# Narrower TensorE tiles, two running totals and split transfers in a kernel of attention, windowed attention and two convolutions

## The chip, the cores and the metric

The kernel runs on one core of a Trainium2 chip. The metric is the device time of one execution in microseconds (us). Before the change the median of three runs is 2969.88 us (2968.04 to 2971.42).

## The reference

Two layers work on `x` of shape (2, 256, 64, 64), in float32. The first is full attention over the 4096 positions of an image, with 8 heads of 32 channels, and a fusion that a mask blends with the input:

```python
attn = softmax(einsum('bnd,bmd->bnm', q / sqrt(32), k))
fuse = einsum('bnm,bmd->bnd', attn, v)
hybrid = conv1x1(concat([x, fuse]), Wf, bf)
x = hybrid * m + x * (1 - m)
```

The second layer has a channel gate, attention inside windows of 8x8 positions (4 heads of 64 channels) with an output projection and a residual, a shuffle of the channels, two grouped 7x7 convolutions (four channels into one, one into four) with normalisation, and a gate:

```python
x = x * sigmoid(relu(x @ ca_w1 + ca_b1) @ ca_w2 + ca_b2)
x = x + (softmax(qw @ kw.T / 8) @ vw) @ out_w + out_b     # per window
y = relu(bn1(conv7x7(shuffle(x), sa_w1)))                 # 64 groups
x = shuffle(x) * sigmoid(bn2(conv7x7(y, sa_w2)))          # 64 groups
```

## The kernel before, in words

**First part (lines 366 to 507).** It projects q, k and v for 16 chunks of 512 positions (8 a image) and keeps them in DRAM, and prepares the banded weights of the two convolutions, the mask and the constants. This part isn't changed.

**Attention (the loop at 1163).** It has 1024 slots: image b, chunk c, half g of the heads (4 heads each), block m of 128 keys (32 blocks). In a slot TensorE makes the scores of the slot two ahead (`scores`, 626: eight matmuls in tiles of 32 rows by 64 columns, written 32*64), ScalarE takes their exponentials in three instructions (639) into a buffer `e` (8 of them), TensorE multiplies the slot's exponentials by the values (`products`, 658: four matmuls in tiles of 128*32 side by side, summed in PSUM over the 32 blocks), and VectorE adds the exponentials to a running total (660). An fp32 matmul stands in the trace as two records, one for each pass. `products` ends a half with a copy of its sum (668). The list `later` holds what is due some slots after: DN = 8 slots after a chunk's end the `denominators` (681: totals times ones, in 128*32), then the reciprocal (706), four transfers of the inverse to DRAM (693) and eight that spread it back over partitions (699), all on GpSimd's queue, and the product with the sum (710).

**The stage of a chunk (`stage`, 714)** is a generator of some dozen pieces. The loop runs one piece every fourth slot, right after a slot's products: fusion with the input (725, first half from `x`, second half from the attention's `f`), `ca1` and `ca2` of the channel gate (754, 768), two q/k projections (796), window scores (830), the v projection (882), transposes (905), outputs (924), the output projection (946), and the sum that goes to DRAM as rows of `x_s` (972) for the convolutions. Fusion, q/k, v and output projection use tiles of 128*128, ca1 128*64. The stages of chunks 0 to 14 run within attention, that of chunk 15 after it.

**Convolutions (`convolve`, 985)**, also a generator. `items` lists 24 pieces of work: 8 groups of channels of image 0 (items 0 to 7, the early ones, whose rows are in DRAM before the end of attention), 6 of image 1 (8 to 13), 8 of both images at once, "pairs" (14 to 21), and two more of image 1. An item loads weights (1010) and rows (1017) on SyncE's queue, makes the first convolution (1038, 56 matmul records, 128*32) and its relu (1046), the second one (1062, 56 records, 32*128, reading weights with a stride of seven elements), tanh and scaling on ScalarE (1072, 1078) into a buffer `z` (two of them), the gate (1084, VectorE), and 12 stores an image (1097). The stores go to GpSimd and SyncE in turn; those of items 4 to 7, once the last stage is through (`staged`), go to GpSimd alone, and those of the last item to ScalarE and SyncE. One step of the generator is a second convolution, or a gate with the first convolution two items on. The order at the end of attention: first convolutions of items 0 and 1, denominators, second convolution of item 0, then the stage of chunk 15 with one convolution step after each piece that says so (`yield True`), then the rest of the items (1193 to 1204).

[...] A second branch of the program, for large scores, isn't taken with these inputs.

Of the kernel before, what the change touches and what calls it, by code (L numbers as in the profile page):

```python
# [10 lines left out]
F32 = mybir.dt.float32  # L11
# [37 lines left out]
UW = UG * KS  # L49
EPS = 1e-5  # L50
SCALE0 = 1.0 / math.sqrt(HD0)

# [4 lines left out]
def conv_seq_kernel(ctx: ExitStack, tc: tile.TileContext, a, out):  # L57
# [37 lines left out]
    for h in range(HEADS0):  # L95
# [12 lines left out]
    inv_s = {  # L108
        (b, c): dram.tile([HEADS0, CH], F32, name=f"invs_{b}_{c}")
        for b in range(B)  # L110
# [403 lines left out]


    def pipeline(arm, shifted, pools):
        fp, xpool, gp, wp, avp, ctx_conv = pools
# [129 lines left out]
        def products(i):  # L647
            b, c, g, m = slots[i]
            if m == 0:
                acc[0] = avp.tile([P, CH], F32, tag="av", name=f"av{arm}_{i}")  # L650
                acc[1] = ep.tile([P, HG, CH], F32, tag="sum", name=f"sum{arm}_{i}", bufs=3)
                totals[b, c, g] = acc[1]
            av, total = acc[0], acc[1]
            e, v = es[i], vts[b, c, g, m // PB]
            start, stop = m == 0, m == NMB - 1
            for j in range(HG):
                r = slice(32 * j, 32 * j + 32)
                nc.tensor.matmul(av[r, :], v[:, m % PB, r], e[:, j, :], start=start, stop=stop)  # L658
            if m > 0:
                nc.vector.tensor_add(total, first[0] if m == 1 else total, e)  # L660
            e = es.pop(i)
            if start:
                first[0] = e
            if stop:
# [25 lines left out]

                def store_inv():
                    for q in range(4):
                        nc.gpsimd.dma_start(  # L693
                            inv_s[b, c][:, q * P : (q + 1) * P], inv[32 * q : 32 * q + HEADS0]
                        )

                def spread(gg):
                    for h in range(HG):
                        nc.gpsimd.dma_start(  # L699
                            rd[32 * h : 32 * h + 32, gg].rearrange("p q n -> p (q n)"),  # L700
                            inv_s[b, c][HG * gg + h].partition_broadcast(32),
                        )
# [3 lines left out]
                at(DN + 1, lambda: nc.vector.reciprocal(inv, inv))  # L706
                at(DN + 1, store_inv)
                for gg in range(KC):
                    at(DN + 1, lambda gg=gg: spread(gg))
                at(DN + 7 + late, lambda: nc.vector.tensor_mul(f, f, rd.rearrange("p g q n -> p g (q n)")))  # L710
# [3 lines left out]
        def stage(b, c):  # L714
# [7 lines left out]
            for half in range(2):  # L722
                for oc in range(KC):
                    for kc in range(KC * half, KC * half + KC):
                        nc.tensor.matmul(  # L725
                            s[:, oc, :],
                            wf[:, kc, oc * P : (oc + 1) * P],
                            f[:, kc - KC, :] if half else xw[kc],
                            start=(kc == 0),
                            stop=(kc == 2 * KC - 1),  # L730
                        )
# [20 lines left out]
            for kc in range(KC):  # L752
                for h in range(2):
                    nc.tensor.matmul(
                        s[64 * h : 64 * h + 64, 0, 0:half],
                        cw1[:, kc, :],
                        x1[:, kc, toks[h]],
                        start=(kc == 0),
                        stop=(kc == KC - 1),
                    )  # L760
# [30 lines left out]
            def project(hc):  # L791
                s = psum2(f"qk{tag}_{hc}")
                for j in range(2):
                    o = (KC * j + hc) * P
                    for kc in range(KC):
                        nc.tensor.matmul(  # L796
                            s[:, j, :],
                            wqkv[:, kc, o : o + P],
                            u[:, kc, :],
                            start=(kc == 0),  # L800
                            stop=(kc == KC - 1),
                        )
# [77 lines left out]
            for t in range(4):  # L880
                for kc in range(KC):
                    nc.tensor.matmul(  # L882
                        sv[:, t, :],
# [60 lines left out]
            for oc in range(KC):  # L944
                for kc in range(KC):
                    nc.tensor.matmul(  # L946
                        s[:, oc, :],
# [34 lines left out]
        items += [(u, (0, 1)) for u in range(EARLY, NU)] + [(1, (1,)), (0, (1,))]  # L982
        staged = []

        def convolve():
            nb = len(BLOCKS)


            early, xcs, ycs = [], [], []
            for k in range(4):  # L990
                early.append(cpool.tile([P, nb, UG, WP], F32, name=f"xe{arm}{k}"))
            for k in range(2):
# [60 lines left out]
            def conv2(k):  # L1053
# [5 lines left out]
                for d in range(KS):  # L1059
                    for j in range(4):  # L1060
                        r = slice(32 * j, 32 * j + 32)
                        nc.tensor.matmul(  # L1062
                            tiles[j // 2][:, j % 2, 0 : n * W],
                            w[r, d],
                            y[r, 0:n, d : d + W],
                            start=(d == 0),
                            stop=(d == KS - 1),
                        )
                z = pool.tile([P, 4, B * nb * W], F32, tag="z", name=f"z{arm}{k}", bufs=2)
                z = z[:, :, 0 : n * W]  # L1070
                for hh in range(2):
                    nc.scalar.activation(  # L1072
                        z[:, 2 * hh : 2 * hh + 2, :],
                        tiles[hh][:, :, 0 : n * W],
                        AF.Tanh,
                        scale=0.5,
                    )
                nc.scalar.activation(z, z, AF.Copy, bias=0.25, scale=0.25)  # L1078
                return z.rearrange("p j (n x) -> p j n x", x=W)

            def gate(k, z):
                u, images = items[k]
                x = xs[k][:, 0 : nb * len(images), :, PAD : PAD + W]
                nc.vector.tensor_mul(z, z, x.rearrange("p n g x -> p g n x"))  # L1084

                engines = (nc.gpsimd, nc.sync)
                if k == len(items) - 1:
                    engines = (nc.scalar, nc.sync)
                elif staged and k < EARLY:
                    engines = (nc.gpsimd,)  # L1090
                stores = 0
                for m, b in enumerate(images):
                    for n, (x0, r0, r1) in enumerate(BLOCKS):
                        for i in range(4):
                            p = 32 * i + 1 - x0
                            stores += 1
                            engines[stores % len(engines)].dma_start(  # L1097
                                dst[b, i, r0:r1, UG * u : UG * u + UG, :],
                                z[p + r0 : p + r1, :, nb * m + n, :],
                            )  # L1100


# [60 lines left out]
        for i, (b, c, g, m) in enumerate(slots):  # L1163
            now[0] = i
            if (b, c, g, m) == (B - 1, NCHUNK - 1, 0, 0):
                for _ in banded:
# [27 lines left out]
        while later:  # L1194
            now[0] += 1
            run_later()
            if now[0] == len(slots) + DN:
                next(conv)
# [91 lines left out]
```

## Time and profile before

| | |
|---|---|
| median of three runs | 2969.88 us |
| the profiled execution | 2969.57 us |
| its span (first to last instruction) | 2967.5 us |
| granted TensorE clock, mean | 0.995 |
| last records of attention's products | 2729.4 us after the start |
| end of the output projection of chunk 15 | 2797.3 us |
| end of the last second convolution | 2954.6 us |

The page of a profile gives, for each engine, its busy time, the chain of work that ended last, and groups of equal instructions: line, engine, operation, written and read tiles, shape, count, then busy time in us and the mean of one in ns, and the idle time of the engine just before them with what ended it. PE is TensorE's matmuls, PEld its weight loads, DVE VectorE, ACT ScalarE, POOL GpSimd, SP SyncE, and SPq its queue. The timeline merges neighbours: start and length in us, and how many records; in brackets the idle time before. Ends of matmuls are modelled, so the starts are read: the distance from one group's start to the next one's is what a group takes. The tail's order on the page:

```profile
PE   9999999999999999999999999999999999999997
...
PEclk9999999999999999999999999999999999999998
DMA  8545421322242324242322223232323232422564
GB/s 248 199 165 172 128 70 53 85 68 78 56 89 63 89 60 89 63 79 70 75 71 68 77 64 75 60 85 62 88 63 74 73 83 66 109 69 78 152 197 103
```

Each of the 40 slices is 74 us: TensorE is busy throughout, and transfers matter at both ends only.

### The profile page before, as it was taken

What the parts mean: (1) busy time and instruction counts of PE and PEld (TensorE: products, weight loads), DVE (VectorE), ACT (ScalarE), POOL (GpSimd) and SP (SyncE); (2) the same over time, 40 slices, a digit from 0 to 9 for tenths busy, and PEclk for the clock granted to TensorE, in tenths of its full rate; (3) what the DMA queues carried; (4) which work ended last, traced back from release to release, by engine and by line L of the source; (5) the groups of instructions that cost most, each with busy time, mean ns of one, the idle gap of its engine ahead of it and who ended that gap; (6) DMA issues with size and microseconds to landing.
All of it is one profiled execution on the core that took longest, in us unless ns stands there. A gap on an engine that the chain in (4) does not pass through costs nothing.

```text
span 2967.5 us, 77160 instructions
## 1 busy us (share of the span) xinstructions
PE 2927.6 (99%) x33162; PEld 915.5 (31%) x33162; DVE 2502.4 (84%) x1348; ACT 2459.3 (83%) x4119; POOL 361.9 (12%) x658
## 2 busy tenths in 40 slices
PE   9999999999999999999999999999999999999997
PEld 3551222222222222222222222222222222223775
DVE  3349999999999999999999999999999999998211
ACT  5569889898989898989989898989898998987333
POOL 8010000000010101010100000010101010000456
PEclk9999999999999999999999999999999999999998
DMA  8545421322242324242322223232323232422564
GB/s 248 199 165 172 128 70 53 85 68 78 56 89 63 89 60 89 63 79 70 75 71 68 77 64 75 60 85 62 88 63 74 73 83 66 109 69 78 152 197 103
DMA packets 230160, 275.74 MB, mean 93 GB/s; under 512 B 116968, under 2 KB 134204, under 8 KB 229552
## 3 DMA queue, kind: packets, MB, share of 16 engines
q1 hardware_dynamic: 200880, 231.47, 27.2%
q0 software_dynamic: 24560, 36.53, 6.0%
q8 instruction: 263, 4.31, 0.6%
q10 hardware_dynamic: 4368, 2.70, 0.3%
q14 instruction: 89, 0.73, 0.1%
HBM read 221.88 MB, written 66.39 MB: 97 GB/s over the span
## 4 chain that ended last, share of the span: by engine, by line
PE 92%; DVE 3%; POOL 2%; DMA 1%; ACT 1%; issue 1%; SPq 0%; DVEq 0%; ACTq 0%; POOLq 0%
PE sa L626 35%; PE ava L658 33%; PE qka L796 4%; PE hya L725 4%; PE q L427 2%; PE vwa L882 2%; DVE suma L660 2%; PE k L427 2%; PE opa L946 2%; PE v L464 2%; POOL out_dram L1097 2%; PE c2a L1062 1%; PE dna L681 1%; DMA out_dram<-za 1%; PE c1a L1038 1%
## 5 line engine op out<-in xcount | busy, mean ns | idle before, releaser
L660 DVE TENSOR_TENSOR suma<-suma,ea 128x2048 f32<-128x2048 f32 x960 | 2198.8, 2290 | 89.9 <-ACT ea L639 3.7
L639 ACT ACTIVATE ea<-sa 128x512 f32<-128x512 f32 (+1 forms) x3072 | 2038.0, 745 | 66.2 <-PE sa L626 25.6
L626 PE MATMUL sa<-qa,ka 32*64 32x512 f32 x16384 | 1157.2, 613 | 1.5 <-ACT vst L472 1.2
L658 PE MATMUL ava<-ea,va 128*32 128x512 f32 x8192 | 1091.2, 605 | 1.3 <-ACT fa L668 0.3
L626 PEld LDWEIGHTS sa<-qa,ka 32*64 32x64 f32 x16384 | 247.5, 129 | 784.5 <-ACT ea L639 718.2
L658 PEld LDWEIGHTS ava<-ea,va 128*32 128x32 f32 x8192 | 161.5, 108 | 834.4 <-issue 805.4
L972 POOL DMA_DIRECT2D xs<-xo x94 | 66.3, 712 | 1718.2 <-DVE xo L957 1713.7
L1097 POOL DMA_DIRECT2D out_dram<-za x210 | 117.8, 569 | 82.4 <-DVE za L1084 56.7
L1084 DVE TENSOR_TENSOR za<-za,xla 128x768 f32<-128x768 f32 (+1 forms) x16 | 21.7, 1359 | 115.6 <-ACT za L1078 75.8
L796 PE MATMUL qka<-ua,qkv_w 128*128 128x512 f32 x256 | 118.4, 605 | 0.0
L660 DVE TENSOR_TENSOR suma<-ea,ea 128x2048 f32<-128x2048 f32 x32 | 73.0, 2283 | 51.3 <-ACT ea L639 51.3
L693 POOL DMA_DIRECT2D invs<-inva x64 | 32.7, 518 | 659.2 <-DVE inva L706 486.3
L1062 PE MATMUL c2a<-yca,wa 32*128 32x192 f32 (+1 forms) x1344 | 101.0, 443 | 8.8 <-ACT za L1072 8.8
L1072 ACT ACTIVATE za<-c2a 128x384 f32<-128x384 f32 (+1 forms) x48 | 26.2, 595 | 97.0 <-DMA out_dram<-za 71.9
L733 ACT ACTIVATE ta<-hya,bf 128x512 f32<-128x512 f32 x32 | 20.2, 683 | 103.7 <-PE hya L725 97.5
L446 DVE TENSOR_REDUCE top<-sq 128x512 f32<-128x2048 f32 x16 | 36.6, 2285 | 79.0 <-ACT sq L440 79.0
L1062 PEld LDWEIGHTS c2a<-yca,wa 32*128 32x128 f32 x1344 | 92.0, 315 | 19.4 <-issue 9.6
L851 ACT ACTIVATE ewa<-ewa,mxwa 128x64 f32<-128x64 f32 x256 | 85.2, 347 | 1.5 <-DVE mxwa L842 1.5
L809 ACT ACTIVATE qka<-qka,qkv_b 128x512 f32<-128x512 f32 x64 | 40.4, 683 | 42.1 <-PE qka L796 41.7
L796 PEld LDWEIGHTS qka<-ua,qkv_w 128*128 128x128 f32 x256 | 46.0, 189 | 71.3 <-issue 46.1
L699 POOL DMA_DIRECT2D rda<-invs x128 | 63.3, 502 | 30.5 <-DMA invs<-inva 30.5
L427 PE MATMUL q<-x,WqT 128*128 128x512 f32 x128 | 61.0, 620 | 5.4 <-DMA WqT<-in_WqT_dram 5.4
(135 smaller groups left out, 1540.5 us busy)
## 6 DMA issues: line engine op xcount, KB each, us to landing
ka<-ks SPq DMA_DIRECT2D x256, 256.0 KB
va<-vs SPq DMA_DIRECT2D x256, 256.0 KB
wa<-ws SPq DMA_DIRECT2D x17, 896.0 KB
ws<-zeros SPq DMA_DIRECT2D x16, 896.0 KB
xs<-xo POOLq DMA_DIRECT2D x78, 140.0 KB, 6.5
xla<-xs SPq DMA_DIRECT2D x24, 420.0 KB
x<-in_x_dram SPq DMA_DIRECT2D x16, 512.0 KB
qs<-qst SPq DMA_DIRECT2D x16, 512.0 KB
```

The lines of the kernel that those rows point to most:

```text
L427: nc.tensor.matmul(s[:, g, :], w[:, kc, g * P : (g + 1) * P], rhs, start=(kc == 0), stop=(kc == KC - 1),)
L626: nc.tensor.matmul(heads[j][o], k[r, cols][:, o], q[r, g, :], start=True, stop=not shifted)
L639: nc.scalar.activation(e[:, h, :], tile, AF.Exp, scale=SCALE0)
L658: nc.tensor.matmul(av[r, :], v[:, m % PB, r], e[:, j, :], start=start, stop=stop)
L660: nc.vector.tensor_add(total, first[0] if m == 1 else total, e)
L699: nc.gpsimd.dma_start(rd[32 * h : 32 * h + 32, gg].rearrange("p q n -> p (q n)"), inv_s[b, c][HG * gg + h].partition_broadcast(32),)
L725: nc.tensor.matmul(s[:, oc, :], wf[:, kc, oc * P : (oc + 1) * P], f[:, kc - KC, :] if half else xw[kc], start=(kc == 0), stop=(kc == 2 * K ...
L796: nc.tensor.matmul(s[:, j, :], wqkv[:, kc, o : o + P], u[:, kc, :], start=(kc == 0), stop=(kc == KC - 1),)
L851: nc.scalar.activation(e[:, n, :], e[:, n, :], AF.Exp, bias=mx[:, n : n + 1], accum_out=rs[:, n : n + 1],)
L972: eng.dma_start(x_s[b, n, p + r0 : p + r1].rearrange("r g w -> g r w"), xo[64 * h : 64 * h + 64, oc, r0 - WS * c : r1 - WS * c, :],)
L1062: nc.tensor.matmul(tiles[j // 2][:, j % 2, 0 : n * W], w[r, d], y[r, 0:n, d : d + W], start=(d == 0), stop=(d == KS - 1),)
L1097: engines[stores % len(engines)].dma_start(dst[b, i, r0:r1, UG * u : UG * u + UG, :], z[p + r0 : p + r1, :, nb * m + n, :],)
```

## The change

- *32-column stage tiles.* The stage's fusion, ca1, q/k, v and output projections call `by_columns`, which splits each matmul into several of 32 output columns (tiles of 128*32).
- *Second convolution in 32*64.* Each of its matmuls is split in two halves of 64 output columns.
- *Two totals.* Exponentials of even and odd key blocks are added to two totals, and these are added at a half's end. The second total lies in a new tile `room`, which the rows of the early items use later; so the last chunk keeps one total, and `convolve` begins 12 slots later in that chunk.
- *Split transfers.* The inverse's layout in DRAM is changed so that one transfer spreads it for both halves of the heads: four stores and four spreads in place of four and eight. For the last chunk they alternate between SyncE and GpSimd.
- *Order.* One more convolution step (the gate and stores of item 0, loads, the first convolution of item 2) is issued ahead of chunk 15's fusion.
- *Gate buffers per image.* `z` holds one image's part, with four buffers; tanh, scaling and gate are done image by image.
- *Stores.* Items 4 to 7 put half of their stores on ScalarE, as do the last two items. Stores for ScalarE are held until after the next second convolution's activations (`held`).

```diff
+    def by_columns(out, weights, x, start, stop):
+        for o in range(0, weights.shape[-1], 32):
+            nc.tensor.matmul(
+                out[o : o + 32], weights[:, o : o + 32], x, start=start, stop=stop
+            )
...
+            chains = 1 if (b, c) == (B - 1, NCHUNK - 1) else 2
...
-            if m > 0:
-                nc.vector.tensor_add(total, first[0] if m == 1 else total, e)
             e = es.pop(i)
-            if start:
-                first[0] = e
+            if m < chains:
+                first[m] = e
+            else:
+                total = acc[1 + m % chains]
+                nc.vector.tensor_add(total, first.pop(m % chains, total), e)
+            if stop and chains == 2:
+                nc.vector.tensor_add(acc[1], acc[1], acc[2])
...
-                def spread(gg):
+                def spread(engines):
                     for h in range(HG):
-                        nc.gpsimd.dma_start(
-                            rd[32 * h : 32 * h + 32, gg].rearrange("p q n -> p (q n)"),
-                            inv_s[b, c][HG * gg + h].partition_broadcast(32),
+                        engines[h % len(engines)].dma_start(
+                            rd[32 * h : 32 * h + 32].rearrange("p g q n -> p (g q n)"),
+                            inv_s[b, c][h].rearrange("g q n -> (g q n)").partition_broadcast(32),
                         )
...
+                queues = (nc.gpsimd,)
+                if (b, c) == (B - 1, NCHUNK - 1):
+                    queues = (nc.sync, nc.gpsimd)
...
-                        nc.tensor.matmul(
+                        by_columns(
                             s[:, oc, :],
                             wf[:, kc, oc * P : (oc + 1) * P],
...
-                        nc.tensor.matmul(
-                            tiles[j // 2][:, j % 2, 0 : n * W],
-                            w[r, d],
-                            y[r, 0:n, d : d + W],
...
+                        for o in HALVES:
+                            nc.tensor.matmul(
+                                tiles[j // 2][o, j % 2, 0 : n * W],
+                                w[r, d, o],
+                                y[r, 0:n, d : d + W],
...
-                z = pool.tile([P, 4, B * nb * W], F32, tag="z", name=f"z{arm}{k}", bufs=2)
...
+                for m in range(len(images)):
+                    z = pool.tile([P, 4, nb * W], F32, tag="z", name=f"z{arm}{k}_{m}", bufs=4)
...
+                while held:
+                    held.popleft()()
+                return zs
...
-                if k == len(items) - 1:
-                    engines = (nc.scalar, nc.sync)
-                elif staged and k < EARLY:
-                    engines = (nc.gpsimd,)
...
+                    if k >= len(items) - 2:
+                        engines = (nc.scalar, nc.sync)
+                    elif staged and k < EARLY:
+                        engines = (nc.gpsimd, nc.scalar)
...
+                            if eng is nc.scalar:
+                                held.append(lambda a=args: nc.scalar.dma_start(*a))
+                            else:
+                                eng.dma_start(*args)
...
-            if (b, c, g, m) == (B - 1, NCHUNK - 1, 0, 0):
+            if (b, c, g, m) == (B - 1, NCHUNK - 1, 0, 12):
...
-            if now[0] == len(slots) + DN:
+            if now[0] in (len(slots) + DN, len(slots) + DN + 1):
                 next(conv)
```

## The prediction

> **What bounds the kernel now.** I read the page first, then the waits, then PE's timeline in one attention stretch and in the tail (all after 2726 us). Times are us.
>
> ```profile
> span 2967.5 us, 77160 instructions
> ...
> PE 2927.6 (99%) x33162; PEld 915.5 (31%) x33162; DVE 2502.4 (84%) x1348; ACT 2459.3 (83%) x4119; POOL 361.9 (12%) x658
> ...
> PE 92%; DVE 3%; POOL 2%; DMA 1%; ACT 1%; issue 1%; SPq 0%; DVEq 0%; ACTq 0%; POOLq 0%
> ...
> L660 DVE TENSOR_TENSOR suma<-suma,ea 128x2048 f32<-128x2048 f32 x960 | 2198.8, 2290 | 89.9 <-ACT ea L639 3.7
> ```
>
> PE is the chain, so what counts is how PE's pieces follow each other. One piece of the fusion stage, one group of denominators, and two slots early on, from PE's timeline:
>
> ```profile
> 317.58 1.47 PE L626 MATMUL sa<-qa,ka 32*64 32x512 f32 x16
> 318.98 1.07 PE L658 MATMUL ava<-ea,va 128*32 128x512 f32 x8
> ...
> 848.25 1.06 PE L658 MATMUL ava<-ea,va 128*32 128x512 f32 x8
> 849.24 3.70 PE L725 MATMUL hya<-xa,WfT 128*128 128x512 f32 x8
> 852.78 3.60 PE L725 MATMUL hya<-fa,WfT 128*128 128x512 f32 x8
> 856.31 1.11 PE L626 MATMUL sa<-qa,ka 32*64 32x512 f32 x16
> ...
> 988.07 1.06 PE L658 MATMUL ava<-ea,va 128*32 128x512 f32 x8
> 988.95 1.93 PE L681 MATMUL dna<-suma,keysum 128*32 128x128 f32 x64
> 990.81 1.11 PE L626 MATMUL sa<-qa,ka 32*64 32x512 f32 x16
> ```
>
> The eight products take 0.99 until a 128*128 piece starts, but 0.88 until the denominators start, which have the products' own tile shape, 128*32: a change of shape costs 0.11. Single records show two more parts: in the 128*128 piece the second matmul starts 0.534 after the first and every later one 0.429 after the one before, so the first weight load costs 0.105; the denominators show no such step. At 317 a slot takes 2.40 (scores 1.40 apart from the products) where it takes 2.04 later; the waits of 280 to 410 say why:
>
> ```profile
> ACT ea L639 <- DVE suma L660: 13.4, 34, 0.7
> ```
>
> The tail, from PE's timeline and the groups by form:
>
> ```profile
> 2750.01 5.43 PE L725 MATMUL hya<-fa,WfT 128*128 128x512 f32 x8 [5.61 <-DVE fa L710]
> 2839.96 4.87 PE L1062 MATMUL c2a<-yca,wa 32*128 32x192 f32 x52 [5.73 <-ACT za L1072]
> 2851.13 2.54 PE L1038 MATMUL c1a<-xla,wa 128*32 128x192 f32 x56
> 2853.60 3.58 PE L1062 MATMUL c2a<-yca,wa 32*128 32x192 f32 x56
> 2949.76 4.86 PE L1062 MATMUL c2a<-yca,wa 32*128 32x192 f32 x52 [3.11 <-ACT za L1072]
> ...
> L1062 PEld LDWEIGHTS c2a<-yca,wa 32*128 32x128 f32 x1344 | 92.0, 315 | 19.4 <-issue 9.6 <-ACT za L1072 9.3
> L1038 PEld LDWEIGHTS c1a<-xla,wa 128*32 128x32 f32 x896 | 34.8, 139 | 21.4 <-issue 17.9 <-ACT za L1072 0.4
> L905 PE MATMUL pta<-ident,ewa 64*64 64x64 f32 x1024 | 18.6, 221 | 0.0
> ```
>
> PE stands still in three places, and each stall is followed by matmuls at a lower clock (5.43 where eight such take 3.60). Between them it is full.
>
> **32-column stage tiles.** In attention each of 15 stages has five pieces whose shape becomes the products' (fusion, two q/k projections, v, output) and ca1. A fusion piece goes from 848.25 to 856.31, 8.06, to 0.88 + 16 passes x 0.429 + 0.12 for the last pass's end (as in the denominators) = 7.87: 0.19 less. The others save the same 0.2 once each, ca1 (64 columns, half the load) 0.15. That is 1.13 a stage, **17.0** for 15, all on PE's chain. The same passes are now four 32-column matmuls side by side. I take 0.429 a pass from the denominators, where such fours follow each other every 0.109 with 0.107 of stream. [...] The denominators' row contradicts it here: 110 ns loads on the same rows, and 2 ns over the stream. I go with the row.
>
> **Two totals.** The adds, dependent, start 2.396 apart (2.29 plus 0.104 idle); an instruction that doesn't need the add before it starts 2.209 after. Their number stays 31 a group. Only where DVE stops ACT does this pay: 291 to 390, before stages give DVE time to catch up. The slots there exceed 2.04 by 11.7 in sum, and ca1 at 406 to 409 waits 1.9 for a late x1. DVE would then lag 0.17 a slot, not 0.36; it hit the limit of eight buffers after 50 slots, and now would after about 100, past the first stage at slot 93. I take **13** (bounds 8 to 15). Elsewhere PE waits nowhere for DVE, so the 11 us a chunk that DVE saves are worth nothing. The last chunk keeps one total; DVE ends it 4.4 after ACT, 1.9 before the denominators need it; that cover stays.
>
> **Second convolution in 32*64.** A pass of one image streams 192 columns, 0.160; it takes 0.230 because the strided load of 128 weight columns does (315 ns, against 139 for 32: 1.8 ns a column plus 0.08). Halves load 64 columns, 0.117, below the stream; first convolutions, four strided loads on the same rows, run at 0.163. So 14 passes shrink from 3.50 to 2.56 each, 16 times; pairs stream 0.320 and save only the first load, 0.12, 8 times. [...] the transposes above make 1024 in 18.6, 18 ns each, so I use the row. Bounds: 0 to 0.95 an image.
>
> **Split transfers and order in the tail.** Denominators end at 2737.2 as before. The inverse's 4 stores and 8 spreads leave POOL at 0.5 each, with two landings (1.6 and 2.3); with 2 + 2 on POOL beside as many on SP, the product with f comes at 2746.0, not 2750.0. The moved step puts item 0's gate, its 12 stores, a row and weight load and item 2's first convolution (2.47) ahead of fusion; its stores queue behind the spreads on both queues, and DVE's gate ends by 2742.6, so nothing waits for them. PE then stands still 0.5, not 5.6, and keeps its clock. Fusion ends at 2749.7, not 2755.4. Through ca1 and ca2 (their chain of ACT and DVE unchanged) the q/k projection starts at 2758.2, not 2764.8; from there to the end of the output projection it was 32.4, which loses a first convolution (2.47), 0.95 of each of two second ones and 0.7 of changed shapes, and gains item 4's second convolution (2.56) and some 0.5 of waits for ACT, busier there: 30.4. The projection ends at 2788.6, not 2797.3 (**-8.7**).
>
> **Gate buffers and stores on ScalarE.** POOL issues all stores of items 4 to 7 (0.57 each), and its backlog to 2837 makes the stall at 2840. Half go to ACT, about 0.43 each. What is queued behind them: as built, each SP or ACT transfer waits for the one eight before it on their shared semaphores. Item 4's last three stores on ACT thus wait for the first three row loads of image 1, and behind them on ACT stands item 7's relu, which frees the one bank that item 8's first convolution needs. Those loads landed 12.7 to 15.1 after the output projection's end (SP issues them at 2807.0 since the rows must be in DRAM first). So PE, out of work 10.0 after that end, waits until 16.0, and loses some 2 more at a low clock; item 7's second convolution ends at 22.9. From there to the last second convolution: six images 2.56, five first 2.47, eight pairs 4.75 + 4.76, two more of each single, 1.5 for short waits: 115.5. Sum 138.4, where before it is 157.3 (2797.3 to 2954.6, stalls included): **-18.9**. At the end the gate no longer waits for the stores of two items back, but item 22's six held stores now stand before item 23's on ACT: 11.4 from the last matmul to the end, not 12.9: **-1.5**.
>
> **Sum.** 17.0 + 13 + 8.7 + 18.9 + 1.5 = 59.1. The profiled execution took 2969.57 (2.1 around its span): 2910.5. The median of the runs, 2969.88, is 0.3 above it. **Forecast 2910**.
>
> **Rivals.**
> - *Conv2 stays load-bound* [...]. For it: 512 columns a pass stay 512. Against: first convolutions. About 14 single items on the path lose 0.95: 2924.
> - *Transfers bind items 8 to 13.* Rows of two images, weights and stores are 2.0 MB an item there; SP was busy 6.3 of 5.97 a step at 2854 to 2867, and a step shall take 5.0. For it: that row; against: row loads run four items ahead and pairs give 9.5 us each. With 1.3 lost at six steps and the stores on ACT later still: 2922.
> - *ACT is not held up*, because the loads come sooner: 2 to 8 less, 2903.
> - *Slower: exposed loads on shared rows*, in the stages' 900 passes, 0.108 each: 2910 + 97 = 3007. It decides from 0.066 a pass (59.1/900). Against: the denominators.
>
> **Chances.** Forecast 0.45, conv2 load-bound 0.18, transfers 0.18, ACT free 0.14, slower 0.04, 0.01 near none. The range reaches from ACT free with all of two totals (2896) to conv2 load-bound with the columns' gain halved (2933). Faster than by 0.2% (5.9 us, about what a measurement of this kernel can tell from no change) 0.95, within 0.01, slower 0.04.
>
> **What would show it.** Products to fusion 0.88, and matmul groups 0.429 apart; no slot of 2.40 before 410; second convolutions of 2.6; no stall before fusion's second half; ACT's stores of item 4 with a wait of some 5 us, PE still for about 6 before item 8; no stall before item 23. It is wrong if passes of four exceed 0.44, if second convolutions stay at 3.5, or if SP's loads hold PE in items 12 to 15.

## The result and the profile after

The changed kernel takes 2924.93 us (median of four runs, 2921.04 to 2925.68) where the kernel before, measured beside it, takes 2970.05: ratio 0.9846, interval 0.9829 to 0.9863. That is 45.1 us less. The forecast was 60 less; the range held the time. In a second measurement on another chip the changed kernel took 2928.31 (2925.95 to 2934.47) against 2971.10: ratio 0.9859 (0.9844 to 0.9874). The profiled execution of the first measurement, 2921.04, is the fastest of its four, that of the second, 2929.98, one of the slower. I use both, since what separates them turns out to be part of the answer.

The page of the changed kernel (the q8 row is the queue that carries instructions: packets, MB, share of the 16 DMA engines):

```profile
span 2919.3 us, 85528 instructions
...
q8 instruction: 295, 4.83, 0.7%
...
PE 97%; DMA 1%; ACT 1%; DVE 0%; issue 0%; SPq 0%; POOL 0%; ACTq 0%; DVEq 0%; POOLq 0%
...
L675 DVE TENSOR_TENSOR odda<-odda,ea 128x2048 f32<-128x2048 f32 x420 | 959.4, 2284 | 50.6 <-ACT ea L646 50.6
```

The same row of the page of before:

```profile
q8 instruction: 263, 4.31, 0.6%
```

DVE's 3% of the chain are gone, and the second total appears, now waiting for ACT and not ACT for it. TensorE is the chain as before. The program has 8368 instructions more, 8320 of them TensorE's, and the instruction queue moved 32 more packets. In attention PE's timeline shows a piece of fusion and two early slots:

```profile
316.03 1.06 PE L669 MATMUL ava<-ea,va 128*32 128x512 f32 x8
317.02 1.11 PE L633 MATMUL sa<-qa,ka 32*64 32x512 f32 x16
318.07 1.06 PE L669 MATMUL ava<-ea,va 128*32 128x512 f32 x8
...
832.76 1.06 PE L669 MATMUL ava<-ea,va 128*32 128x512 f32 x8
833.64 3.62 PE L519 MATMUL hya<-xa,WfT 128*32 128x512 f32 x32
837.08 3.62 PE L519 MATMUL hya<-fa,WfT 128*32 128x512 f32 x32
840.62 1.11 PE L633 MATMUL sa<-qa,ka 32*64 32x512 f32 x16
```

Products are followed by fusion after 0.88, not 0.99; from products to the next scores it takes 7.86, where before it took 8.06 and the forecast said 7.87. The slot at 316 takes 2.04, not 2.40. The tail, PE's timeline again, where a bracket names what PE waited for:

```profile
2718.33 3.64 PE L519 MATMUL hya<-fa,WfT 128*32 128x512 f32 x32 [1.68 <-DVE fa L727]
...
2772.76 3.76 PE L1082 MATMUL c2a<-yca,wa 32*64 32x192 f32 x107 [1.73 <-issue]
2780.61 4.26 PE L1057 MATMUL c1a<-xla,wa 128*32 128x192 f32 x56 [4.09 <-ACT yca L1065]
2784.80 2.64 PE L1082 MATMUL c2a<-yca,wa 32*64 32x192 f32 x112
2787.37 2.53 PE L1057 MATMUL c1a<-xla,wa 128*32 128x192 f32 x56
```

The stop before fusion's second half is 1.7, not 5.6, and the matmuls behind it keep their clock (3.64). A second convolution of one image takes 2.57 (2784.80 to 2787.37). But there are two stops that before did not have: one that waits for nothing the profile shows ("issue"), five matmuls into item 6's second convolution, and one before item 8, for ScalarE. ScalarE's timeline shows the latter (ACTq is ScalarE's queue issuing transfers):

```profile
2769.01 11.08 ACTq L1128 DMA_DIRECT2D out_dram<-za  x6
2780.14 0.42 ACT L1065 ACTIVATE yca<-c1a,cbias 128x192 f32<-128x192 f32 x1 [10.34 <-DMA xla<-xs]
```

Six stores take 11 us to issue since the last three wait for row loads, and item 7's relu stands behind them: the wait that the prediction described, 10.3 long.

By stretches, each from start to start of the named records in PE's timeline, as differences from before (us):

| from the stretch before to | before | forecast | changed, first measurement | changed, second |
|---|---|---|---|---|
| first scores | 185.2 | 0 | +1.5 | +1.5 |
| last record of attention's products | 2544.3 | -30.0 | -30.6 | -26.3 |
| fusion's second half, chunk 15 | 20.5 | -4.0 | -2.6 | -2.4 |
| last record of the output projection | 46.7 | -4.7 | -2.5 | -1.7 |
| item 8's first convolution | 16.0 | +0.6 | +2.1 | +2.3 |
| last record of the last second convolution | 141.4 | -19.5 | -17.3 | -13.7 |
| end | 13.4 | -1.5 | +1.1 | +1.1 |
| sum | 2967.5 | -59.1 | -48.3 | -39.3 |

Attention came out as forecast where nothing stopped TensorE. That the first profile meets its 30.0 so closely is in part luck: all eleven other profiles with 32-column tiles, the second measurement's among them, lose 1.1 to 5.1 right behind the fourth chunk's denominators, and it loses nothing there. The first part, which isn't changed, takes 1.5 more in both (0.6 to 2.1 over all the variants); its cause stays open. The rest of the miss lies in the tail, and in stops of the kind "issue".

### The profile page after: what moved, and what is told of

Same layout as the page of the kernel before. It is cut to its first block, busy times and chain, and to the rows that moved or that the text cites. A ratio compares the mean times of both kernels' runs of the same rounds, so it can differ in the third digit from the quotient of the medians.

```text
span 2919.3 us, 85528 instructions
## 1 busy us (share of the span) xinstructions
PE 2881.9 (99%) x37322; PEld 837.2 (29%) x37322; DVE 2434.9 (83%) x1356; ACT 2455.9 (84%) x4143; POOL 315.1 (11%) x560
## 4 chain that ended last, share of the span: by engine, by line
PE 97%; DMA 1%; ACT 1%; DVE 0%; issue 0%; SPq 0%; POOL 0%; ACTq 0%; DVEq 0%; POOLq 0%
PE sa L633 37%; PE ava L669 35%; PE hya L519 4%; PE qka L519 4%; PE c2a L1082 2%; PE q L428 2%; PE c1a L1057 2%; PE opa L519 2%; PE vwa L519 2%; PE v L465 2%; PE k L428 2%; PE dna L695 1%; PE sca L847 1%; PE pta L922 1%; PE oa L941 1%; PE ca2a L785 1%
## 5 line engine op out<-in xcount | busy, mean ns | idle before, releaser
L675 DVE TENSOR_TENSOR suma<-suma,ea 128x2048 f32<-128x2048 f32 x480 | 1097.4, 2286 | 5.7 <-ACT ea L646 0.5
L675 DVE TENSOR_TENSOR odda<-odda,ea 128x2048 f32<-128x2048 f32 x420 | 959.4, 2284 | 50.6 <-ACT ea L646 50.6
L519 PE MATMUL qka<-ua,qkv_w 128*32 128x512 f32 x1024 | 115.8, 592 | 0.3 <-DVE ua L803 0.3
L1130 POOL DMA_DIRECT2D out_dram<-za x180 | 101.3, 571 | 77.8 <-DVE za L1110 56.3
L1110 DVE TENSOR_TENSOR za<-za,xla 128x768 f32<-128x768 f32 x24 | 23.0, 960 | 94.3 <-ACT za L1099 53.7
L754 DVE TENSOR_TENSOR ta<-ta,mca 128x512 f32<-128x512 f32 x32 | 22.0, 688 | 77.4 <-ACT ta L750 77.4
L1082 PE MATMUL c2a<-yca,wa 32*64 32x192 f32 (+1 forms) x2688 | 83.7, 387 | 2.6 <-issue 2.3
L1093 ACT ACTIVATE za<-c2a 128x384 f32<-128x384 f32 x64 | 27.8, 486 | 57.9 <-PE c2a L1082 41.6
L1082 PEld LDWEIGHTS c2a<-yca,wa 32*64 32x64 f32 x2688 | 64.7, 192 | 22.0 <-issue 12.7
L677 DVE TENSOR_TENSOR suma<-suma,odda 128x2048 f32<-128x2048 f32 x30 | 68.8, 2292 | 1.0
```

Source lines behind the costliest of these rows:

```text
L519: nc.tensor.matmul(out[o : o + 32], weights[:, o : o + 32], x, start=start, stop=stop)
L675: nc.vector.tensor_add(total, first.pop(m % chains, total), e)
L677: nc.vector.tensor_add(acc[1], acc[1], acc[2])
L1082: nc.tensor.matmul(tiles[j // 2][o, j % 2, 0 : n * W], w[r, d, o], y[r, 0:n, d : d + W], start=(d == 0), stop=(d == KS - 1),)
L1130: eng.dma_start(*args)
```

## The experiments

All kernels are variants of the changed one but the first. Ratios are to the kernel before, measured beside each.

| kernel | median us | ratio (interval) | attention | tail after it |
|---|---|---|---|---|
| before | 2970.05 to 2972.72 | 1 | 2544.3 | 238.0 |
| changed | 2924.93 | 0.9846 (0.9829 to 0.9863) | 2513.7 | 218.9 |
| changed, second measurement | 2928.31 | 0.9859 (0.9844 to 0.9874) | 2518.0 | 223.5 |
| before, with columns only | 2957.32 | 0.9943 (0.9926 to 0.9959) | 2532.9 | 237.9 |
| one total | 2941.30 | 0.9897 (0.9880 to 0.9913) | 2528.7 | 225.0 |
| 64-column tiles | 2941.80 | 0.9898 (0.9882 to 0.9915) | 2527.2 | 225.1 |
| second convolution of 128 | 2932.20 | 0.9859 (0.9843 to 0.9876) | 2518.4 | 226.5 |
| stores of items 4 to 7 on GpSimd | 2925.65 | 0.9854 (0.9839 to 0.9869) | 2515.6 | 220.4 |
| ScalarE's stores for the last item only | 2931.23 | 0.9870 (0.9855 to 0.9885) | 2515.5 | 226.9 |
| both of these | 2925.02 | 0.9843 (0.9830 to 0.9857) | 2517.7 | 218.8 |
| last spreads on GpSimd | 2928.30 | 0.9859 (0.9843 to 0.9876) | 2517.3 | 222.4 |
| no extra step | 2930.30 | 0.9865 (0.9848 to 0.9881) | 2515.8 | 224.5 |
| 64 records more | 2928.84 | 0.9860 (0.9843 to 0.9876) | 2517.0 | 220.5 |
| no stores of items 8 to 13 | 2928.68 | 0.9856 (0.9839 to 0.9872) | 2516.1 | 226.7 |

"Attention" runs from the first scores to the last products, "tail" from there to the end, both of the profiled execution.

### What attention gained, and from what

**Columns alone**, on the kernel before: five calls of the stage become `by_columns`.

```diff
-                        nc.tensor.matmul(
+                        by_columns(
                             s[:, oc, :],
                             wf[:, kc, oc * P : (oc + 1) * P],
```

> The kernel before, with only the 32-column stage tiles added. Theory (the changed kernel's chunk period fell from 159.93 to 158.79 us, and this is the columns' doing alone): 15 stages x 1.14 = 17.1, and 0.7 in chunk 15's own stage: 17.8 less than before, about 2952. The slots near 317 stay at 2.40, since nothing helps VectorE. Rival (VectorE takes the place of TensorE: with one total a chunk needs 151.4 of work and 62 gaps of 0.104 between dependent adds, 157.8, all but the whole of a period of 158.8): part of the gain is lost, the period ends between 159.0 and 159.9, and the whole is above 2955.

The period of a chunk is 158.8, as in the changed kernel, and the slots near 317 stay at 2.40. The ratio is worth 16.9 us, the medians 15.4. The profile's own gain in attention is 11.4 only, because TensorE stops there once for 2.43 ("issue", at 832) and runs slower for a few slots after (products take 1.33 and 1.34, not 0.99). The theory holds and its rival, VectorE as the new bound, falls: from the third chunk on the period is 158.79, but for the chunk with the stop (163.85) and one of 159.07.

**One total**, in the changed kernel:

```diff
-            chains = 1 if (b, c) == (B - 1, NCHUNK - 1) else 2
+            chains = 1
```

> The changed kernel with one running total in every chunk. Theory (the second total matters only in the first chunk, where no stage gives VectorE time to catch up): the slots from about 290 to 390 take 2.40 again, 13.5 us come back, about 2934.5 for a profiled execution of 2921.0; the chunk period stays at 158.8. Rival (with the shorter period VectorE's chain of dependent adds, 157.8 a chunk, sets the pace, or delays f and x1): the period grows too, by up to 1 us in each of 15 chunks, and the kernel is above 2940.

Attention is 15.0 longer; 11.7 of it are slots of the first chunk that take 2.40 again, 2.2 come with the late x1 before ca1, 1.1 with a slower group of scores at 828 (more on that place below). The period of the other chunks stays at 158.8. ScalarE's wait is the one of before, to the digit:

```profile
ACT ea L646 <- DVE suma L675: 13.4, 34, 0.7
```

So VectorE's 11 us a chunk are worth nothing outside the first chunk.

**64-column tiles**, to part the change of shape from the width of the first load:

```diff
-        for o in range(0, weights.shape[-1], 32):
+        for o in range(0, weights.shape[-1], 64):
```

> The changed kernel with stage tiles of 64 columns (128*64), not 32. Theory (a stage piece gains mainly because its tiles have the shape of the products' tiles, so that the change of shape at 0.113 falls away; the narrower first load is the smaller part): 6 pieces a stage x (0.113 + 0.027), 15 stages: 12.6, and 0.5 in the last stage: about 2934; products before a stage piece take 0.99 again. Rival (the width of the first load is all that counts): 6 x 0.027 x 15 = 2.4: about 2923.5, and products before a stage piece stay at 0.88.

PE's timeline of this kernel:

```profile
836.06 1.06 PE L669 MATMUL ava<-ea,va 128*32 128x512 f32 x8
837.06 3.65 PE L519 MATMUL hya<-xa,WfT 128*64 128x512 f32 x16
```

Products take 0.99 again before a stage piece (1.00 from the rounded starts). Attention is 13.5 longer than in the changed kernel's first profile, where 12.6 was expected and the rival said 2.4; a period is 159.7. What narrow tiles buy here is that six pieces a stage no longer change the tile shape; the shorter first load is the small part.

### What the second convolution gained

```diff
-                        for o in HALVES:
+                        for o in (slice(0, P),):
```

> The changed kernel with second convolutions of 128 output columns again. Theory: 16 convolutions of one image go from 2.57 back to 3.50 and 8 of two images from 4.80 to 4.88; of the 15.6 some 2 lie under the waits before fusion's second half and before item 8: 13 to 14 more, about 2934. Rival (the doubled matmuls cost instruction loading: the changed kernel's two stops of TensorE inside second convolutions that wait for nothing visible, 1.73 and 0.55, with a low clock after, come from them): these go away, and the loss is 9 to 10, about 2930.

A convolution of one image is 3.50 again, and yet neither number came. By ratio the kernel equals the changed one of the second measurement and is 3.9 behind that of the first, with intervals that overlap: the times alone don't show that the halves gain. By stretches it is 1.5 to 2.4 slower up to the output projection, 0.3 to 0.5 faster from there to item 8's first convolution, 1.0 to 4.0 slower from item 8's to item 14's, 2.4 to 3.0 from there to the last record, and 1.4 faster at the end: 3.0 to 7.6, of the 14 that the forecast gave. The lost part has two places. The second convolutions of items 5 and 6 lie under the wait before item 8, which follows the output projection in either kernel (17.8 and 18.0 after it). And in items 8 to 13 TensorE's own work fell from 6 x (2.47 + 3.50) = 35.8 to 30.2, but the stretch only from 38.3 to 34.3 or 37.2. In between the convolutions follow each other at TensorE's own 2.57 and 2.47 (2784.80 to 2809.99 is five steps of 5.04); what is lost lies at the two ends. Slow matmuls after the stop before item 8 take 1.7 and 2.8 (2.4 in this kernel too), the "issue" stop in item 13's second convolution, with slow matmuls behind it in the second profile, 1.2 and 3.9, and in the first profile a wait before item 14 takes 1.2. No "issue" stop stands in this kernel's tail, so that part of the rival was right; but two stand in its attention (1.88 and 1.34), which the rival did not foresee.

### The wait before item 8, and the end

The changed kernel again, as measured beside the three variants that follow:

> The changed kernel once more, as a reference for the three others on the same chip. Its profiled execution took 2921.0 where its other runs took 2924.5 to 2925.7. Theory: the profiled one had fewer or cheaper stops; the stop before fusion's second half (1.68) and the one before item 8 (4.1 of TensorE's waiting) were 2.2 to 2.3 and 5.1 to 6.5 in two variants with the same tail. Expected here: about 2924, the stop before item 8 between 4 and 6.5, attention's own part (first scores to last products) at 2508.9 unless TensorE stops there for something the profile doesn't show.

The stop before item 8 is 3.5 (4 to 6.5 expected) and the one inside item 6 is 2.1; attention takes 2518.0, by a measure that gives 2513.7 for the first profile; it has a stop of 1.68 at 818, where the first profile had none. It came out above the expected 2924, at 2928.31: the stops differ from one execution to the next, and the first profile caught few.

```diff
-                        engines = (nc.gpsimd, nc.scalar)
+                        engines = (nc.gpsimd,)
```

> The changed kernel with the stores of items 4 to 7 on GpSimd alone, none on ScalarE. Theory (item 8's first convolution waits for item 7's relu, which stands behind ScalarE's stores, and these wait for row loads on the same semaphores): the stop before item 8 ends when its own rows land, some 15 after the output projection's end, not 18.2; it is below 2 and the clock stays up: 4 to 5 less, about 2920 median, and with four gate buffers GpSimd's backlog (6.9 a item against steps of 5) reaches no stall. Rival A (the rows themselves are late; ScalarE's wait only runs beside it): within 1.5 of the changed kernel. Rival B (GpSimd's backlog holds the gate buffers, as before the change): a stop of 3 to 6 before a second convolution in items 9 to 12, slower than the changed kernel or equal.

```profile
2779.46 4.19 PE L1057 MATMUL c1a<-xla,wa 128*32 128x192 f32 x56 [2.06 <-DMA xla<-xs]
...
2816.49 6.48 PE L1057 MATMUL c1a<-xla,wa 128*32 128x384 f32 x56 [2.46 <-DMA xla<-xs]
```

In PE's timeline of this kernel item 8's first convolution comes 15.1 after the output projection, not 18.2, and waits for its own rows, not for ScalarE. So ScalarE's stores did hold it, by 3. But the stop of 2.06 is no shorter than the 2 expected, and the clock didn't stay up behind it (4.12 to the next start, 2.47 at full clock). GpSimd's backlog holds ScalarE's tanh once, for 4.7, but stops no second convolution (rival B falls). The stretch to item 14 is 37.0, much as in the changed kernel's second profile and 2.7 more than in its first, and ends in a wait for rows. The median is 2.7 below the changed kernel's, well inside the intervals.

```diff
-                    if k >= len(items) - 2:
+                    if k == len(items) - 1:
```

> The changed kernel with ScalarE taking stores only for the last item, as in the kernel before; item 22's go to GpSimd and SyncE. Theory (24 stores of the last two items stand on two queues, and each waits for the one eight before it): the time from the last second convolution to the end falls from 14.4 to about 11, 3 less, about 2921.5 median. Rival (the end is set by the last gate and the landing of its own stores): no change within 1, since the last item's six stores a queue and their landing stay.

This theory fell: the end takes 18.3, not 11, and in the next kernel, with the same edit, 13.8. GpSimd's queue is no free place. It issues item 21's twelve stores one after the other at 0.53 to 0.60 each, and item 22's six start at 2912.7, though their gate ended at 2910.7. The changed kernel's 14.6 are 2.9 until ScalarE issues its first store, 7.1 for its twelve (six took 3.05 before) and 4.6 from there to the end; with six (5.3 here) the end came no sooner, so that what must go to shorten it stays open.

> The changed kernel with both edits: stores of items 4 to 7 on GpSimd alone, and ScalarE's stores only for the last item. Theory: the two gains add, since they lie in different places: 7 to 8 less than the changed kernel, about 2917 median. Rival (a later start of item 8 was covered by transfers that bind items 8 to 13): the sum is 3 to 4 only.

The tail is 218.8 in this profile, 4.7 below the changed kernel's second and equal to its first. By median it is 3.3 less: the rival's 3 to 4, not the theory's 7 to 8, but the intervals overlap, so I can't call it faster. No version here beats the changed kernel beyond doubt.

### What comes before fusion

```diff
-                    queues = (nc.sync, nc.gpsimd)
+                    queues = (nc.gpsimd,)
```

> The changed kernel with the inverse's four stores and four spreads of the last chunk all on GpSimd's queue. Theory (each costs GpSimd 0.55, so two queues save some 2.2 in the chain from the reciprocal to f): TensorE's stop before fusion's second half grows from 1.7 to 2.1 to about 4, the clock then drops and fusion's second half takes 5.4 where it took 3.6: 4 more, about 2929 to 2932. Rival (the landings alone count, and SyncE's transfers land no sooner than GpSimd's): within 1 of the changed kernel, the stop stays at 2.

PE's timeline of this kernel, and then of the changed one in the second measurement:

```profile
2722.90 5.34 PE L519 MATMUL hya<-fa,WfT 128*32 128x512 f32 x32 [2.87 <-DVE fa L727]
```

```profile
2722.73 3.64 PE L519 MATMUL hya<-fa,WfT 128*32 128x512 f32 x32 [1.83 <-DVE fa L727]
```

The stop grows by 1.0 (2.2 expected), and the clock drops as expected, which costs 1.7. From attention's end to the output projection it is 2.3 to 3.2 more, yet the median equals the changed kernel's of the second measurement: this is as far as the times can tell.

```diff
-            if now[0] in (len(slots) + DN, len(slots) + DN + 1):
+            if now[0] == len(slots) + DN:
```

> The changed kernel without the extra convolution step ahead of chunk 15's fusion. Theory (item 2's first convolution, 2.47, lies under the wait for f): the stop grows by 2.5 to above 4, the clock drops for fusion's second half (1.8), and the convolution is paid later: 4 more in all, about 2929 to 2932. Rival (item 0's twelve stores no longer share queues and DMA engines with the spreads, and f comes sooner): the stop grows by less than 1.5, and the whole by 1 to 2.

The stop is 3.67 and fusion's second half takes 6.2 to the next start. f itself comes 0.3 to 0.5 sooner, so the rival has a little truth, but the stop grew by 1.8 to 2.0. Up to the output projection it is 1.9 to 2.8 more; the median is 2.0 above that of the second measurement. The step is worth about half of the 4 expected.

### The stops that wait for nothing

Counted in matmul records from the start, "issue" stops come after the same number in kernel after kernel: at 34416 in the changed kernel, in both measurements, and in five variants of the same length; at 8599 in nine of the kernels with columns (the one with columns only among them, whose tail is another; in seven of the nine the profile names ScalarE's exponentials there instead of "issue"); at 33906, 35437, 35182 and 35692 in some. Their distances, 510, 1021, 766, 255 and so on, are multiples of 127 to 128 records. With its weight load a record is two instructions (the page counts 37,322 of each), so the distance is 255 to 256 instructions, and TensorE's 74,644 of them, with 506 semaphore instructions, make 294 such pieces, where the instruction queue moved 295 packets (before: 66,324 and 435, 261 pieces, 263 packets). To test that these numbers, and not the work at these places, make the stops, I shifted the stream by 64 records:

```diff
-                    for h in range(HEADS0):
+                    twice = (b, c) == (0, 1)
+                    for h in [*range(HEADS0)] * (2 if twice else 1):
```

> The changed kernel with the denominators of chunk 1 computed twice (64 matmul records more, the same values). TensorE's stops that wait for nothing visible came after the same number of matmul records in every run (8599, 34416, also 33906 and 35437). Theory (these are ends of loaded pieces of the instruction stream, about 128 records of matmuls with their weight loads): they come after the same numbers again, 8599 and 34416 of the new count, 64 records sooner in the work, if they come at all; a stop that waits for data stays at its work (item 8's first convolution, number 34587). Rival (something in the work at these places stops TensorE): 8663 and 34480. Time: 1.9 more for the doubled group, and stops of 0 to 2 each gained or lost.

PE's timeline of this kernel:

```profile
816.74 2.70 PE L633 MATMUL sa<-qa,ka 32*64 32x512 f32 x16
...
2782.84 4.71 PE L1058 MATMUL c1a<-xla,wa 128*32 128x192 f32 x56 [8.20 <-ACT yca L1066]
...
2814.05 2.20 PE L1058 MATMUL c1a<-xla,wa 128*32 128x192 f32 x46 [1.85 <-issue]
```

No stop stands at 8599, 8663, 34416 or 34480. One stands at 35437 of the new count, after ten matmuls of a first convolution, where that number before meant the 19th matmul of a second one. A shorter one (0.60) stands at 35310, 127 records ahead of it. The wait before item 8 moved with its work, to 34587. So in the tail the number decides, as the theory has it, on two stops of one execution. For the stop in attention the rival isn't out: the group of scores right behind the fourth chunk's denominators, inside which number 8599 lies in the other kernels, still loses 1.6 here (2.63 to the next start where it takes 1.04), at records 8664 to 8675, where no piece ends. The gain is eaten at once: without the stop in item 6 TensorE runs out of work sooner and waits 8.2 before item 8, not 3.5; the time is that of the changed kernel.

That data transfers make these loads late was tested by leaving out stores:

```diff
+                            if EARLY <= k < EARLY + 6:
+                                continue
                             eng = engines[stores % len(engines)]
```

> The changed kernel leaving out the stores of items 8 to 13, so that those rows of the output are not written. Theory (stores, rows and instructions share the DMA engines, and the six items lose 4 to 7 above TensorE's own 30.2 to it): from item 8's to item 14's first convolution 32 instead of 34.3 to 37.6, no stop inside items 8 to 13 and none before item 14. Rival (the row loads alone, 0.42 MB an image and 0.84 for the first pair, come too late): the stop before item 14 stays at 1 to 2.8, and the stretch at 34 or more.

```profile
2807.70 0.64 PE L1082 MATMUL c2a<-yca,wa 32*64 32x192 f32 x13 [2.15 <-issue]
...
2825.91 2.19 PE L1057 MATMUL c1a<-xla,wa 128*32 128x384 f32 x23 [1.35 <-issue]
```

The theory falls. The stretch to item 14 takes 38.7, with "issue" stops of 2.15 and 0.94 in it and one of 1.35 right behind. The wait for rows before item 14 is gone, but TensorE also comes to it later than in the kernels that wait, so this doesn't show that the stores made those rows late. Without stores ahead of them on SyncE's queue the rows of the coming items go out in one go (two loads of a pair in 0.89 where the changed kernel needed 2.4 to 4.1).

The traces' packets of the instruction queue (16,384 bytes each) show the rest. The tails have 34 "issue" stops above 0.4, in eleven profiles, and each ends 1.2 to 1.6 after the end of such a packet. Each stands at the end of a piece, counted in 256 of TensorE's instructions. A packet begins about when TensorE enters a new piece (in attention the median difference is 0.13 or less); the packet ahead of each of the 34 stops began 1.0 to 5.7 late, 3.0 in the median, while TensorE used its piece up in 2.6 to 4.6 (6.3 in two). In these spells packets of the other queues kept the 16 DMA engines busy for 91% of the time in the median (41% and more), against 50 to 56% from 2700 to 2830. In the kernel without stores, from 2800 on, all of it was SyncE's queue with rows and weights. So the stops of the tail go with instruction packets that start late while other transfers run; what makes the packets late, no run isolates. The seven stops at 8599 that name ScalarE end 2.0 to 3.8 after a packet and don't fit this: their cause stays open.

## Why the prediction was right or wrong

**32-column tiles: right.** Period 158.79 for 159.93, 15 x 1.14 = 17.1 for a forecast of 17.0. The four side by side follow each other every 0.429, on shared rows, where a load takes 110 ns, so the slower rival's exposed loads (0.108 a pass, 97 in sum) did not appear in the stage pieces, no more than in the denominators before the change; that rival rested on a supposition that no trace here showed.

**Two totals: right.** 13.5 (30.6 less 17.1) for 13, and one total gave back 13.9 in the same places, the slots of the first chunk and the late x1.

**Second convolution: the duration right (2.57 for 2.56, 3.50 before; pairs 4.80 for 4.76), its worth wrong.** The sum took the saving of items 8 to 13 as paid in full. The stretch has 4.1 and 7.0 above TensorE's own 30.2. That isn't the transfers' rival, which loses 1.3 at each of six steps: steps take their 5.0, and the excess is the low clock after the stop before item 8 and one "issue" stop, with one wait in the first profile. The prediction's own sign of being wrong, SP's loads holding PE in items 12 to 15, came in part: before item 14 TensorE waits 1.2 in the first profile and 1.4 to 2.8 in six variants, for rows or, by the profile, for a store on SyncE's and ScalarE's shared semaphores; not in the second profile. And the measured 2924.93 lies at the number of another rival, second convolutions that stay load-bound (2924); with 2.57 each they don't, so that this agreement is luck.

**Split transfers and order: mechanism right, sizes off.** Fusion's second half began 1.4 to 1.6 later than forecast: GpSimd's two spreads landed 3.4 to 3.6 after their issue (3.7 to 3.8 in the second measurement), where I had taken 2.3. The output projection lost another 2.2 to 3.0 of its gain, 1.1 to 1.4 of it to an "issue" stop inside the transposes (0.64 and 1.18 with slower matmuls behind), the rest in waits of a few tenths.

**Stores on ScalarE: right.** The wait for the row loads, what is behind it and who waits for that are as described. TensorE ran dry 13.4 (14.1 in the second measurement) after the output projection, not 10.0, since the "issue" stop and its low clock fell into that time, and item 8 started 1.4 to 1.6 late.

**The terms that were mis-sized** most are the last two. "1.5 for short waits" between item 7's second convolution and the last one measured 3.6 and 6.2: the parts of that sum were right (they add up to 115.35, not 115.5), what lies between them was not. "11.4 from the last matmul to the end, not 12.9" measured 14.2. I named item 22's six stores ahead of item 23's on ScalarE and then took a gain from the gate none the less; the last two items' stores took ScalarE from 2907.6 to 2914.6 to issue, 7 us for the last item's 3.1 of before. Behind a good part of the first, and of what was lost ahead of item 8, stands a cost that the prediction did not have at all: 4160 more matmul records came with 32 more packets of instructions, and 43 records a us in a halved convolution (112 in 2.57) use a piece of 128 up in 3 us, where attention (24 in a slot of 2.04) takes 11. The runs show stops of 0.4 to 2.4 at some of the crossings from one piece to the next, 2.9 in sum in the first profile (2.3 in second convolutions, 0.6 in transposes) and 7.3 in the second measurement's (4.4, 1.2, and the 1.7 in attention whose cause is open), without the low clock behind them. Part of that is covered, as the shifted stream showed.

## What to carry to other kernels

Cost an edit by the distance from start to start of the pieces in the stage where it acts, and then ask what else paces that stage: the same halved convolution was worth most of its price from item 14 on (2.4 to 3.0; by durations, three times 0.93 and eight times 0.08 make 3.4), and 1.0 to 4.0 of 5.6 in items 8 to 13, where instruction packets came late. Splitting matmuls into more instructions had a price here that no group's row shows: 32 more packets of instructions, and "issue" stops of 2.9 us in sum in the first profile. Look at the instruction queue's packets and for "issue" stops at equal distances. A stop that is removed ahead of another wait is worth only what that wait leaves over, so take the waits of a tail in their order.

## What the runs showed of the hardware

A stop of TensorE can cost more than its length. In seven profiles fusion's second half came after a stop of 1.11 to 1.83 and took 3.64; in six after one of 2.13 and more (2.13, 2.23, 2.31, 2.87, 3.67 and 5.68) it took 5.34 to 6.45. In the 5.3 us after the stop of 2.87 the granted clock was 0.68, in the 3.6 after that of 1.83 it was 1.00. After the stop before item 8 it was 0.50 in the second measurement. An edge near 2 us holds for this place only. The first row below, of the kernel with both edits of the stores, follows a stop of 1.42 in attention and has products at half speed; the second, of the kernel with its stores on GpSimd, follows a stop of 2.03 in item 6 and runs at full clock:

```profile
819.55 1.94 PE L669 MATMUL ava<-ea,va 128*32 128x512 f32 x8
```

```profile
2774.80 2.60 PE L1082 MATMUL c2a<-yca,wa 32*64 32x192 f32 x107 [2.03 <-issue]
```

The granted clock is 1.00 or 0.50 in every profile, and until the last matmul each low stretch lasts 3.41, 6.83 or 10.24 us. In a profile the low stretches begin whole multiples of 3.41 apart (819.05, 2778.30, 2785.13 and 2819.26 in the second measurement). So the length of a stop alone doesn't tell whether the clock drops.

A change of tile shape from 128*32 to 128*64 costs the same 0.11 as one to 128*128: products take 1.00 and 0.99 before these, 0.88 before a piece of their own shape.
